# A graph-attention kernel on one core: a new written order for the steady slot, and 13 of 28 projection half passes back to 128 columns

## The chip, the cores and the metric

The kernel runs on 1 core of one Trainium2 chip. The metric is the time on the device in microseconds (us) of one execution. A core has five engines with queues of their own: TensorE (PE; its weight loads are listed as PEld), VectorE (DVE), ScalarE (ACT), GpSimd (POOL) and SyncE (SP, which only issues DMA transfers here). Each executes its own instructions in the order in which the program lists them, and waits on semaphores for the others.

## The reference

For each of 32 batches `b`, `x[b]` is 512 channels by 1024 nodes in float32. What is computed, cut to what matters:

```
q = wq . x          k = wk . x                    # per node
s[m, n] = leaky_relu(q[n] + k[m], 0.01)
att = softmax(s, over n)                          # 1024 x 1024 per batch
agg[c, m] = sum_n x[c, n] att[m, n]
y = layernorm(x + relu(adj @ agg + bm))           # layer 0; norm over the nodes
W = adj * adj
out = layernorm(y + W^T y + bias)                 # layer 1
```

## The kernel before, in words

**The attention without its matrix.** Because of leaky_relu, exp(s) is a product of a function of q and one of k on each side of a threshold. The kernel ranks the nodes by q, stores the projected rows z = (q, adj·x, k) in rank order in DRAM, makes prefix sums of exp(q)·z from both ends ("tables"), stores them too, and each node then fetches one row of three entries (prefix, own rank's row, suffix) and mixes them.

**The steps.** Everything that a batch needs is cut into named steps, and a text lists the steps of one "slot". In a slot several batches are at different stages: a step has a role (an offset to the slot's number), so slot s does the projection of batch s+2, the tables and fetches of batch s+1, the mixing and the layer-1 product of batch s, the last layernorm of batch s-1, and loads batch s+3. The list is the order in each engine's queue. One slot after the other makes the steady part. Names, in the order of one batch:

- `ld0..3` load x (SP). `x01..x04`, `x11..x14` (DVE, 128x512 subtractions and additions): operands of a Strassen-like product with seven products per half g; their place is in `y` for g = 0 and in rows 0 to 3 of the tile `rows` for g = 1.
- `p0..p27` (PE, L312, `project`): 28 half passes of 2 products with contraction 128, 257 columns moving. Results are collected in PSUM tiles of the tags A, B and C (each one buffer of two banks; T is the fourth tag). `k0p1 k0p5 k0u2 k021 k1...` (ACT, L333) and `k011 k012 k022 k111 k112 k122` (DVE, L331) bring them to `zrow`. `p12` can't write tag C before `k011` has read it, and `p15` can't write A before `k022`.
- `pk mx mr qb ql en`: maximum of q, q on all partitions (PE transposes). `r0..r7` (DVE, L377): ranks. `sd0..sd7` (POOL, L389): indirect DMA of `zrow` to DRAM in rank order. `fe` (SP, L435 and L440): the ranked rows back into `zs`, after all eight `sd`. `c0..c7` (ACT, L402): counts for each k.
- `wx0 wx1` (ACT, L450) and `wb0 wb1` (DVE, L462): weights of the tables, from the first column of `zs`. `t0..t8` (PE, L484, 64 columns): the tables, one after the other in tag T (`t8` in C); `e` (ACT, L496) reads each out, `ca` (ACT) and `cp` (POOL, L502) carry one row to the next, `ts` (SP, L510) stores it, by two DMAs.
- `pi0..pi7` (POOL, L517, indirect DMA into `rows`): each node's row, after the landing of all `ts`. `oa`, `no` (DVE, L532 on, L546 on), `ox`, `sh`, `sx`: the mixing factors; `oa0` needs `pi0` to `pi3`, `oa1` needs `pi4` to `pi7`. `sc` (ACT, L556) and `ga`, `gb` (DVE, L561): the mixing itself, for 8 groups of rows.
- `u0..u3` (PE, L568): 8 transposes each of all rows, so `u0` is behind the last `ga`/`gb`. They use tag C, so each waits for the `ad` of the one before. `ad` (DVE, L575), `sq` (ACT), `rt` (POOL), `y` (ACT, L600): layer 0's sum and layernorm.
- `T1..T4` (DVE, L624), `sA sB` (PE, L630, bias seeds), `m0..m13` (PE, L647, 128x128 weights, 512 columns moving), `rd...` (ACT L670, DVE L668): layer 1 by seven products.
- `st ro sf av so`: statistics (DVE), root (POOL), shift (DVE), application (ACT), store (SP).

**The half passes.** A product in `project` is made as two matmuls of 64 weight columns each, which go to the two halves of the output partitions:

```
        for c in range(2):
            for n in range(0, P, G):
                nc.tensor.matmul(
                    zp[n : n + G, m, 0:CE],
                    side(b, g, a)[:, c, m * P + n : m * P + n + G],
                    wb[:, w, c, :],
```

with P = 128, G = 64 and CE = 257. In the profile each float32 matmul shows as two records, so a half pass has 8 records.

**Order around it.** `begin()` and `opening()` make the first three batches' work by hand up to the first slot, `slot(s)` runs the list for s = 1 to 29 (the first copy of the list is run by `opening()`), and `end()` the last two batches by hand.

Of the kernel before, what the change touches and what calls it, by code (L numbers as in the profile page):

```python
# [23 lines left out]
def gat_gcn_resnorm_kernel(  # L24
# [141 lines left out]
    def turn_weights():  # L166
        pt = bank("T", [P, N], "pt_v")
        nc.tensor.transpose(pt[:, 0 : 3 * CT], vec, ident[0 : 3 * CT, 0 : 3 * CT])
        for i in range(2):
            nc.vector.tensor_copy(wb[:, 2 * i + 1, :, 0], pt[:, 2 * i : 2 * i + 2])  # L170
            nc.vector.tensor_copy(wb[:, 2 * i, :, CE - 1], pt[:, CT + 2 * i : CT + 2 * i + 2])
        nc.vector.tensor_scalar(nbm, pt[:, 2 * CT : 3 * CT], -1.0, None, ALU.mult)
        for ct in (2, 3, 0, 1):
            pt = bank("ABCT"[ct], [P, C], f"pt_{ct}")
            for ot in range(CT):
                nc.tensor.transpose(
                    pt[:, ot * P : (ot + 1) * P], adj_sb[:, ot, ct * P : (ct + 1) * P], ident
                )
            i = 2 * (ct // 2)
            nc.vector.tensor_copy(wb[:, i, ct % 2, 0 : CE - 1], pt[:, C // 2 : C])  # L180
            nc.scalar.copy(wb[:, i + 1, ct % 2, 1:CE], pt[:, 0 : C // 2])
        for to, of, less in ((4, 1, 0), (5, 3, 4), (6, 2, 5), (1, 3, 1)):
            nc.vector.tensor_tensor(wb[:, to], wb[:, of], wb[:, less], ALU.subtract)

    def seed_bias():
# [18 lines left out]
    def square_weights():  # L204


        nc.vector.scalar_tensor_tensor(w1, adj_sb, SC, adj_sb, ALU.mult, ALU.mult)
        for ct in range(CT):
            w = w1[:, ct, ct * P : (ct + 1) * P]
            nc.vector.scalar_tensor_tensor(w, ident, SC, w, ALU.mult, ALU.add)  # L210
        nc.vector.tensor_tensor(ws[:, 0], a21, a22, ALU.add)
        nc.vector.tensor_tensor(ws[:, 1], ws[:, 0], a11, ALU.subtract)
        nc.vector.tensor_tensor(ws[:, 2], a12, ws[:, 1], ALU.subtract)
        nc.vector.tensor_tensor(a21, a11, a21, ALU.subtract)
# [89 lines left out]
    def project(b, i):  # L304
# [4 lines left out]
        zp = held(zps, (b, g, at), lambda: bank(at, [P, 2, H], f"zp_{at}_{b}_{g}"))  # L309
        for c in range(2):  # L310
            for n in range(0, P, G):
                nc.tensor.matmul(  # L312
                    zp[n : n + G, m, 0:CE],
                    side(b, g, a)[:, c, m * P + n : m * P + n + G],
                    wb[:, w, c, :],
                    start=first and c == 0,
                    stop=c == 1,
                    skip_group_check=not first,
                )
# [26 lines left out]
    def spread(b, to="T"):  # L346

        qb = qbs[b] = bank(to, [P, N], f"qb_{b}")
# [216 lines left out]
    def turn(b, ot, at="C"):  # L565
        op = tops[b, ot] = bank(at, [P, N], f"op_{b}_{ot}")
# [139 lines left out]

    steps = {}
# [56 lines left out]
    for what in names:  # L764
        also(0, f"rd{what}", read, what)

# [10 lines left out]
    def run(s, plan, but=()):  # L777

        for name in plan.split():
            if name not in but:  # L780
                do(s + steps[name][0], name)

    def tables(b, *some):
        for k in some:
            do(b, f"t{k} e{k}")
            if k < NB - 1:
                do(b, f"cp{k} ca{k}")
            do(b, f"ts{k}")

    def gains(b, *some):  # L790
        do(b, " ".join(f"{g}{k}" for g in ("ga", "gb") for k in some))

    kept = {
        3: "k0p1 k011", 5: "k0p5", 7: "k0u2", 9: "k012", 11: "k022", 15: "k021",
        17: "k1p5", 19: "k1p1 k111", 23: "k1u2 k112", 25: "k122", 27: "k121",
    }

    def whole(b, before={}, after={}):

        do(b, "x01 x02 x04 x03 x11 x12 x14 x13")  # L800
        for i in range(NP):
            for f in before.get(i, ()):
                f()
            do(b, f"p{i} {kept.get(i, '')}")
            for f in after.get(i, ()):
                f()

    def begin():

        turn_weights()  # L810
        whole(0)
        square_weights()
        do(0, "pk")
        spread(0, "B")
        done.add(("qb", 0))
        do(0, "mx mr ql en")
        do(0, "r0 r1 sd0 sd1 r2 r3 sd2 sd3 r4 r5 sd4 sd5 r6 r7 sd6 sd7 fe")
        seed_bias()
        whole(
            1,  # L820
            before={
                21: (lambda: do(0, "wx0 wb0"),),
                24: (lambda: tables(0, 0),),
                26: (lambda: tables(0, 1), lambda: do(0, "wx1 wb1")),
            },
            after={
                i: (lambda z=z: do(0, f"c{z}"),) for z, i in enumerate((3, 7, 10, 14, 17, 21))
            },
        )
        do(1, "pk")  # L830
        spread(1, "B")
        done.add(("qb", 1))
        do(1, "mx mr ql en")

        def pair(nt):
            do(1, f"r{nt} r{nt + 1} sd{nt} sd{nt + 1}")

        def gather():
            do(0, "pi0 pi1 pi2 pi3")
            do(1, "fe")  # L840
            do(0, "pi4 pi5 pi6 pi7")

        whole(
            2,
            before={
                0: (lambda: pair(0), lambda: tables(0, 2), lambda: do(0, "c6")),
                2: (lambda: pair(4), lambda: tables(0, 3), lambda: do(0, "c7")),
                4: (lambda: pair(2), lambda: tables(0, 4), lambda: do(0, "sh sx")),
                5: (lambda: pair(6), lambda: tables(0, 5)),
                7: (lambda: tables(0, 6),),  # L850
                9: (lambda: tables(0, 7),),
                11: (lambda: tables(0, 8),),
                12: (gather,),
                13: (lambda: do(1, "c0 c1"),),
                16: (lambda: do(1, "c2 c3"),),
                19: (lambda: do(1, "c4 c5"),),
                23: (lambda: do(1, "c6 c7 wx0 wb0"),),
                25: (lambda: tables(1, 0),),
                27: (lambda: tables(1, 1),),
            },  # L860
        )

    def shares(b, h):
        do(b, f"oa{h} ox{h} no{h} " + " ".join(f"sc{k}" for k in range(4 * h, 4 * h + 4)))

    def opening():

        shares(0, 0)
        do(1, "wx1 wb1")
        gains(0, 0, 1)  # L870
        tables(1, 2)
        gains(0, 2, 3)
        tables(1, 3)
        shares(0, 1)
        gains(0, 4, 5, 6, 7)
        do(1, "sh sx")
        for ot in range(CT):
            turn(0, ot, "CA"[ot % 2])
            done.add((f"u{ot}", 0))
            tables(1, 4 + ot)  # L880
            do(0, f"ad{ot} sq{ot} rt{ot}")
            if ot > 0:
                do(0, f"y{ot - 1}")
# [185 lines left out]
```

## Time and profile before

| | us |
|---|---|
| median of 3 runs | 2316.03 (2310.62 to 2318.45) |
| the profiled execution | 2319.07 |
| its span, from first to last instruction | 2317.4 |
| PE busy | 2141.9 (92%) |
| DVE busy | 1806.8 (78%) |
| ACT busy | 1648.0 (71%) |
| POOL busy | 1020.2 (44%) |
| mean granted TensorE clock | 0.973 of full speed; 1.00 in the ten windows of the steady part that were looked at |

Some groups of instructions, by line and shape (mean ns of one):

| step | shape | count | mean ns |
|---|---|---|---|
| p, zp_A from x, L312 matmul | 128 rows, 64 columns, 257 moving | 2048 | 387 |
| p, its weight load | 128x64 | 2048 | 138 |
| t, L484 matmul | 128 rows, 64 columns, 257 moving | 2304 | 402 |
| m, oA from y, L647 matmul | 128x128, 512 moving | 768 | 601 |
| m, its weight load | 128x128 | 768 | 192 |
| u, L568 transpose | 128x128, 128 moving | 1024 | 283 |
| u, its weight load | 128x128 | 1024 | 143 |
| ga, gb, L561 | 128x512 | 512 | 778 |
| st, L676 (two per step) | 128x512 | 240 | 676 |
| r, L377 | 128x1024 | 240 | 1281 |
| sd, L389 | indirect DMA | 256 | 1252 |
| pi, L517 | indirect DMA | 256 | 1079 |

Matmul records overlap, and their ends are modelled: what a step costs on PE is read from the distance of starts, not from the mean duration. "Busy" for PE is therefore no measure of how close it is to its limit. A slot can be marked by the first transposes of L568, which occur once in a slot behind all mixing; in the time from 255 us to 2155 us the single transpose of L357 (step `mx`) returns every 66 to 71 us.

### The profile page before, as it was taken

The numbers are of one execution on the slowest core, as the hardware profiler recorded it, in microseconds if no ns is written. First come the engines' busy times: TensorE is split into PE (matmuls) and PEld (weight loads), VectorE is DVE, ScalarE is ACT, GpSimd is POOL, SyncE is SP. The second block draws the span as 40 slices with busy tenths as digits, with TensorE's granted clock in tenths as the row PEclk, the third lists the DMA queues.
The fourth block names the chain that finished last, engine by engine and source line by source line (L and its number), as shares of the span: only waits on it lengthen the run. The fifth ranks groups of instructions, "written<-read, shape, count | busy, mean of one in ns | idle before, by whom it ended". The sixth has DMA issues, their size and how long they took to land.

```text
span 2317.4 us, 37553 instructions
## 1 busy us (share of the span) xinstructions
PE 2141.9 (92%) x12689; PEld 1204.2 (52%) x12721; DVE 1806.8 (78%) x3574; ACT 1648.0 (71%) x2758; POOL 1020.2 (44%) x1293
## 2 busy tenths in 40 slices
PE   6669999999999999999999999999999999999776
PEld 4334555555555555555555555555555555555332
DVE  6537888788888888878788878888888888888555
ACT  1357778777777877677787777877777777777654
POOL 1225444444544444455444455444445544444431
PEclk9879999999999999999999999999999999999878
DMA  6357777777877777887777787777778777778641
GB/s 237 95 192 238 259 243 246 239 249 253 270 259 243 247 236 254 248 269 247 236 233 252 239 274 261 240 234 244 244 249 283 258 231 238 249 248 269 223 175 72
DMA packets 178774, 548.96 MB, mean 237 GB/s; under 512 B 27020, under 2 KB 27032, under 8 KB 178584
## 3 DMA queue, kind: packets, MB, share of 16 engines
q1 hardware_dynamic: 121216, 277.05, 40.8%
q0 software_dynamic: 57344, 269.52, 33.2%
q8 instruction: 101, 1.65, 0.3%
q14 instruction: 89, 0.73, 0.1%
q10 hardware_dynamic: 24, 0.01, 0.0%
HBM read 338.17 MB, written 208.30 MB: 236 GB/s over the span
## 4 chain that ended last, share of the span: by engine, by line
PE 39%; DMA 23%; DVE 8%; ACT 7%; issue 7%; POOL 5%; SPq 2%; POOLq 0%; DVEq 0%; ACTq 0%
PE tp L484 11%; DMA rows<-td,idx 11%; PE zp_A L312 10%; PE op L568 6%; DMA zs<-td 5%; PE zp_B L312 4%; PE oA L647 4%; DMA td<-zrow,ranki 3%; POOL rows L517 3%; DMA td<-zs 2%; POOL td L389 2%; DVE st L676 2%; DMA x<-in_x_dram 2%; ACT x L584 2%; DVE rows L561 2%
## 5 line engine op out<-in xcount | busy, mean ns | idle before, releaser
L484 PE MATMUL tp<-zs,lq 128*64 128x257 f32 x2304 | 364.6, 402 | 60.9 <-POOL zs L502 37.4
L389 POOL DMA_INDIRECT td<-zrow,ranki x256 | 320.4, 1252 | 198.2 <-DVE ranki L382 97.1
L561 DVE SCALAR_TENSOR_TENSOR rows<-rows,ra 128x512 f32<-128x512 f32 x512 | 380.4, 778 | 19.1 <-ACT rows L556 15.8
L647 PE MATMUL oA<-y,adj_sb 128*128 128x512 f32 x768 | 352.4, 601 | 6.9 <-DVE v L668 2.4
L377 DVE SCALAR_TENSOR_TENSOR junk<-qb,zrow,first 128x1024 int8<-128x1024 f32 x240 | 307.5, 1281 | 18.1 <-DMA out_dram<-v 7.5
L517 POOL DMA_INDIRECT rows<-td,idx x256 | 276.2, 1079 | 92.7 <-issue 68.0
L312 PE MATMUL zp_A<-wb,x 128*64 128x257 f32 x2048 | 280.9, 387 | 27.5 <-DVE zrow L331 26.0
L502 POOL COPY zs<-ts 1x513 f32<-1x513 f32 x128 | 81.8, 639 | 457.6 <-ACT ts L496 457.6
L484 PEld LDWEIGHTS tp<-zs,lq 128*64 128x64 f32 x2304 | 184.0, 140 | 187.1 <-POOL zs L502 63.6
L575 DVE SCALAR_TENSOR_TENSOR y<-op,nbm,x 128x1024 f32<-128x1024 f32 x128 | 164.0, 1284 | 149.9 <-PE op L568 148.1
L402 ACT ACTIVATE junk<-lq,kc 128x1024 int8<-128x1024 f32 x240 | 274.3, 1143 | 1.9
L647 PEld LDWEIGHTS oA<-y,adj_sb 128*128 128x128 f32 x768 | 145.1, 192 | 190.0 <-issue 149.0
L312 PEld LDWEIGHTS zp_A<-wb,x 128*64 128x64 f32 x2048 | 165.2, 138 | 106.0 <-DVE zrow L331 42.0
L502 POOL COPY zs<-zs 1x513 f32<-1x513 f32 x128 | 78.8, 615 | 268.6 <-ACT zs L496 268.6
L333 ACT COPY zrow<-zp_A 128x514 f32<-128x514 f32 x192 | 112.6, 586 | 112.4 <-PE zp_A L312 94.5
L556 ACT ACTIVATE rows<-rows,ra 128x512 f32<-128x512 f32 x256 | 175.6, 713 | 4.3 <-DVE ra L549 4.3
L670 ACT COPY v<-oA 128x1024 f32<-128x1024 f32 x90 | 89.8, 998 | 107.9 <-PE oA L647 97.2
L600 ACT ACTIVATE y<-y,nb,r 128x1024 f32<-128x1024 f32 x128 | 158.9, 1242 | 4.3
L312 PE MATMUL zp_C<-wb,x 128*64 128x257 f32 x1024 | 147.0, 388 | 15.9 <-DVE zrow L331 15.4
L700 ACT ACTIVATE v<-v,nb,rs 128x1024 f32<-128x1024 f32 x120 | 148.6, 1238 | 13.7 <-DVE nb L692 11.7
L568 PE MATMUL op<-ident,rows 128*128 128x128 f32 x1024 | 148.3, 283 | 9.6 <-DVE rows L561 7.2
L676 DVE BATCH_NORM_STATS2 st<-v 128x6 f32<-128x512 f32 x240 | 152.1, 676 | 0.0
(163 smaller groups left out, 3858.0 us busy)
## 6 DMA issues: line engine op xcount, KB each, us to landing
x<-in_x_dram SPq DMA_DIRECT2D x128, 512.0 KB
out_dram<-v SPq DMA_DIRECT2D x120, 512.0 KB
zs<-td SPq DMA_DIRECT2D x64, 602.3 KB
td<-zs SPq DMA_DIRECT2D x288, 120.2 KB
td<-ts SPq DMA_DIRECT2D x224, 120.2 KB
zs<-td SPq DMA_DIRECT2D x64, 240.9 KB
zs<-td SPq DMA_DIRECT2D x96, 120.5 KB
td<-zs SPq DMA_DIRECT2D x8, 514.0 KB
```

What stands on the lines that cost most here:

```text
L312: nc.tensor.matmul(zp[n : n + G, m, 0:CE], side(b, g, a)[:, c, m * P + n : m * P + n + G], wb[:, w, c, :], start=first and c == 0, stop=c ...
L377: nc.vector.scalar_tensor_tensor(junk(b)[:, 0:N], qbs[b], zrow[:, nt, 0:1], first[:, o : o + N], ALU.subtract, ALU.is_lt, accum_out=rank[: ...
L389: sc = nc.gpsimd.indirect_dma_start(out=td[:, :], out_offset=bass.IndirectOffsetOnAxis(ap=ranki[:, nt : nt + 1], axis=0), in_=zrow[:, nt, ...
L402: nc.scalar.activation(junk(b)[:, N : 2 * N], qs[b], AF.Sign, bias=kcs[b][:, nt : nt + 1], accum_out=signs(b)[:, nt : nt + 1],)
L484: nc.tensor.matmul(tp[i * G : (i + 1) * G, h, 0:CE], lw[:, ks[i], :], zs[:, j, 1 + h * CE : 1 + (h + 1) * CE], start=True, stop=True,)
L517: nc.gpsimd.indirect_dma_start(out=rows[:, mt, :], out_offset=None, in_=tdb[b % 2].rearrange("(s u) c -> s (u c)", u=3), in_offset=bass.In ...
L556: nc.scalar.activation(u, u, AF.Copy, scale=ratios(b)[:, k, 1:2])
L561: nc.vector.scalar_tensor_tensor(u, rg[:, k, i, 1 : C + 1], ratios(b)[:, k, i : i + 1], u, ALU.mult, ALU.add)
L568: nc.tensor.transpose(op[:, mt * P : (mt + 1) * P], rg[:, mt, 1, 1 + ot * P : 1 + (ot + 1) * P], ident)
L575: nc.vector.scalar_tensor_tensor(yall[:, ot], tops.pop((b, ot)), nbm[:, ot : ot + 1], xs[b][:, ot], ALU.max, ALU.add, accum_out=sm,)
L647: nc.tensor.matmul(o[:, m, :], quarters[w][:, a, m * P : (m + 1) * P], part(b, y)[:, a, :], start=fresh and a == 0, stop=a == CT // 2 - 1, ...
L676: nc.vector.bn_stats(st[:, h, :], vs[b][:, mt, h * H : (h + 1) * H])
```

## The change

It replaces the list of the steady slot by another one with the same steps (none is added or left out), and it makes `project` choose its form by a second list: the half passes in `NARROW` keep two 64-column matmuls per product, the other 13 (p1 to p4 and p19 to p27) make one matmul of 128 columns. The hand-written `begin()`, `opening()` and `end()` become lists as well (`BEGIN`, `END`), and helper functions are cut into steps for this; the order of their steps stays, apart from the one copy of the slot's list that each holds, which follows the new list, and `wb0` of the last batch, which goes from POOL to DVE.

```diff
         zp = held(zps, (b, g, at), lambda: bank(at, [P, 2, H], f"zp_{at}_{b}_{g}"))
+        wide = G if f"p{i}" in NARROW.split() else P
         for c in range(2):
-            for n in range(0, P, G):
+            for n in range(0, P, wide):
                 nc.tensor.matmul(
-                    zp[n : n + G, m, 0:CE],
-                    side(b, g, a)[:, c, m * P + n : m * P + n + G],
+                    zp[n : n + wide, m, 0:CE],
+                    side(b, g, a)[:, c, m * P + n : m * P + n + wide],
                     wb[:, w, c, :],
...
     SLOT = """
-    ga3 st1 p4 p1 st0 p3 p2 ga2 ro0 ga0 p0 k0p1 st2 p5 p7 k0p5 gb0 ro2 p6 k011 ro1 sf2 ga1 p12 k0u2
-    st3 av2 p8 p11 oa1 ro3 sf1 p10 ox1 av1 no1 p9 sf0 k022 sc6 sc5 p15 k012 ga5 p14 wx0 wb0 sc4 x11
-    t0 k021 gb1 p19 sf3 e0 gb5 sc7 cp0 ts0 ga6 p17 ca0 ga4 so1 av3 t1 gb2 gb6 p16 e1 wx1 p18 cp1 ts1
-    wb1 ca1 k1p1 t2 x12 gb3 p13 e2 ga7 p23 ca2 cp2 ts2 gb7 av0 k111 t3 k1p5 gb4 u0 e3 p22 ca3 cp3
-    ad0 k1u2 t4 x13 sq0 u1 p24 e4 ld0 ad1 so0 ca4 cp4 p25 so2 rt0 x14 sq1 t5 k122 sh u2 e5 ld1 rt1
-    ts3 y0 p20 ad2 cp5 p21 ca5 sq2 t6 k112 p27 e6 sB ca6 cp6 ts6 u3 y1 rt2 ts5 t7 ad3 so3 ts4 p26 e7
-    pk ld2 mx ca7 cp7 qb ts7 mr k121 sq3 t8 r0 sA r1 e8 m1 rt3 y2 ts8 en ld3 T1 sd0 ql m0 y3 r2 sd1
-    m3 c0 T2 pi2 sx m2 r3 rdp1 pi0 c1 r4 pi3 m5 rdp5 r5 pi1 m7 T3 sd3 m4 r6 r7 m6 rdu2 c2 sd6 m9
-    rd11 c3 sd5 T4 m8 pi7 x01 oa0 m11 pi5 rd22 ox0 c4 no0 sd4 c5 m10 x02 sd7 sc0 m12 c6 x03 sd2 rd12
-    sc3 m13 sc2 pi4 x04 pi6 rd21 sc1 c7 fe
+    ga2 st1 p4 p1 ga3 p2 ga0 st3 p3 p5 k0p1 gb3 ro3 p6 k0p5 st0 p7 st2 p0 ro0 k0u2 p9 gb0 ro2 p10
+    sf3 gb2 ro1 p11 sf0 oa1 av0 k011 p8 k022 ox1 av3 so0 p12 no1 p15 x11 sc5 p14 wx0 wb0 sc4 t0 k012
+    k021 ga1 p17 e0 gb1 ca0 p19 cp0 ts0 ga4 sc6 sf2 x12 t1 sc7 ga5 p16 ga7 e1 p18 wx1 sf1 cp1 ts1
+    wb1 ca1 k1p1 t2 gb7 av2 gb4 p13 e2 ga6 ca2 p23 cp2 k111 av1 gb5 t3 gb6 k1p5 so1 u0 x14 so3 e3
+    so2 ca3 p22 cp3 ad0 t4 k1u2 x13 sq0 u1 p25 e4 ad1 ca4 cp4 ts4 p24 rt0 sq1 t5 u2 e5 rt1 y0 p21
+    ts5 ad2 cp5 p20 ld0 ca5 ts2 k122 sq2 t6 k112 ld1 pk u3 sh e6 ld2 ca6 p27 cp6 ad3 y1 t7 mx p26 e7
+    mr T1 ca7 cp7 ts7 qb sq3 ts6 t8 r0 ts3 sB rt3 e8 r1 m3 k121 ts8 rt2 ld3 en y2 sd0 m2 y3 pi1 sA
+    m1 ql T2 pi2 T3 pi0 m0 r2 pi3 m7 rdp1 r3 rdp5 m5 T4 sd2 c0 r4 pi5 c1 m4 r5 sd1 m6 rdu2 r6 sd3 c2
+    m8 r7 sd4 c3 x01 pi7 m11 c4 oa0 rd11 sd5 ox0 c5 m9 x02 sd7 sx c6 no0 m10 sd6 rd22 sc0 sc2 m12
+    pi6 x03 sc3 x04 pi4 rd12 m13 rd21 c7 sc1 fe
     """
 
+    NARROW = "p0 p5 p6 p7 p8 p9 p10 p11 p12 p13 p14 p15 p16 p17 p18"
```

## The prediction

> **What bounds the kernel now.** First the page, for the span and the slices:
>
> ```profile
> span 2317.4 us, 37553 instructions
> PE 2141.9 (92%) x12689; PEld 1204.2 (52%) x12721; DVE 1806.8 (78%) x3574; ACT 1648.0 (71%) x2758; POOL 1020.2 (44%) x1293
> PE   6669999999999999999999999999999999999776
> ```
>
> PE looks like the bound, and 33 of 40 slices are steady. The timeline of one slot shows where it isn't (PE, then the waits of the other engines):
>
> ```profile
> 1067.66 1.04 PE L350 MATMUL qb<-ident,zrow 128*128 128x128 f32 x8
> 1068.63 1.09 PE L484 MATMUL tp<-zs,lq 128*64 128x257 f32 x8
> 1069.65 0.60 PE L630 MATMUL oA<-seeds,ones 128*128 128x512 bf16 x2
> 1070.09 3.60 PE L647 MATMUL oA<-y,adj_sb 128*128 128x512 f32 x8
> ...
> 1075.83 1.05 POOL L517 DMA_INDIRECT rows<-td,idx  x1 [0.58 <-issue]
> 1079.80 2.05 POOL L517 DMA_INDIRECT rows<-td,idx  x1 [0.30 <-issue]
> 1088.60 0.16 DVE L532 TENSOR_TENSOR s<-rows,kc 128x4 f32<-128x4 f32 x1 [1.44 <-DMA rows<-td,idx]
> 1096.44 1.01 POOL L517 DMA_INDIRECT rows<-td,idx  x1 [0.30 <-issue]
> 1106.57 0.16 DVE L532 TENSOR_TENSOR s<-rows,kc 128x4 f32<-128x4 f32 x1 [2.43 <-DMA rows<-td,idx]
> 1108.93 1.96 PE L312 MATMUL zp_A<-wb,x 128*64 128x257 f32 x16 [2.58 <-DVE zrow L331]
> 1110.09 0.67 ACT L450 ACTIVATE w<-zs,bw,el 128x2 f32<-128x2 f32 x2 [0.36 <-DMA zs<-td]
> 1110.86 1.36 PE L484 MATMUL tp<-zs,lq 128*64 128x257 f32 x8
> ```
>
> And the same slot by stages, from its `u0` (1052.49) on:
>
> ```profile
> 1052.49:1058.49 6.00, 6.00 (x51) 3.99 (x52) 4.23 (x7) 5.03 (x11) 1.59 (x3) 1.00 0.11 10
> 1058.49:1074.49 16.00, 15.95 (x105) 9.81 (x103) 10.76 (x25) 15.32 (x26) 7.03 (x13) 1.00 0.91 309
> 1074.49:1102.49 28.00, 27.61 (x119) 13.42 (x119) 25.28 (x46) 17.95 (x31) 21.17 (x21) 1.00 0.89 308
> 1102.49:1110.49 8.00, 5.42 (x50) 3.36 (x48) 4.87 (x16) 3.86 (x7) 1.44 (x3) 1.00 1.01 214
> 1110.49:1120.20 9.71, 9.64 (x77) 6.28 (x75) 9.53 (x18) 8.09 (x15) 1.88 (x3) 1.00 0.49 144
> ```
>
> (Columns: length, busy PE, PEld, DVE, ACT, POOL, clock, DMA share, GB/s.) PE loses 2.6 us in the fourth stage, where the DMA engines are full (1.01); in the first and last they are nearly free (0.11, 0.49). The slot is a loop through all engines, and I count it from `u0`, averaged over 23 slots, 67.95 us: `u0` to `t8` 16.1 (PE); `e8`, `ts8` and its landing; four fetches on POOL; they land, and `oa0` starts at 36.6. From there DVE has no slack until the last `gb`, and the next `u0` waits for that. Start distances price DVE: `ga`/`gb` 0.70, `st` 1.44, `x` and `k` 0.60, wide adds (`rd`, `T`) 1.15, `oa` 0.56, `no` 0.71, `wb0` 0.50, `wb1` 1.34, `sf` 0.10. In the old order what follows `oa0` sums to 29.5; 36.6 + 29.5 leaves 1.85 of DVE idle in 67.95, which are waits such as the 2.43 above for the last four fetches.
>
> **The change, part by part.**
>
> *The form.* Narrow half passes start 0.87 apart; 8 records in pairs, 0.214 a pair. No 128-column float32 matmul with 257 moving columns is in the trace. By the nearest row, `m` (0.4285 from start to start for 512 columns), a wide record takes 0.215, four of them 0.86: equal. The far end is that the 128-column load (0.192 in `m`) isn't hidden: 4 x (0.214 + 0.192) = 1.62, or 13 x 0.76 = 9.9 us in a slot; below nothing, only the few records less, which PE doesn't wait for. I take 0.86: in `m` each load begins with the matmul before it and has 0.215 to hide in, and `u` has 128x128 loads and matmuls every 0.109.
>
> *The switches.* `qb`, whose neighbour before is wide, lasts 0.97, and `t8` behind it 1.02, where alone they need 0.87 each. Over many pairs a change of form costs about 0.10 before and 0.05 behind: 0.15. The old slot has 12 changes on PE; I count 16 in the new one (`p3`|`p5`, around `p19`, around `p23` are new; `u0`-`p22`, `u1`-`p25` and their like only move them). That is 4 x 0.15 = 0.6 us a slot on PE. The Trainium skill (TensorEngine Tiling, Key Properties) says that changing the tiling mode drains the TensorE. The trace agrees (0.15 a change), and the rule alone speaks against this change; its result is a rival below. I cost the switches at nothing: `p3`|`p5` lies in a stage where PE waits for DVE, and `p19` and `p23` lie between tables `t0` to `t3`, where `t2` waits for `wb1`. Without that cover they cost the 0.6.
>
> *`sB` goes behind `t8`.* The seeds of tag B (0.44) stood in the stretch from `u0` to `t8`, which is PE's alone. `t8`, `e8`, `ts8` are 0.44 earlier. `ts8` is now behind `ts6` and `ts3` on SP; a `ts` holds SP 0.85 (two issues, four took 1.70). `ts7` can go at 14.5 after `u0`, the two are through at 17.1, and `e8` ends at 17.7 (18.14 before): not late.
>
> *Fetches.* POOL's order was `sd0 sd1 pi2 pi0 pi3 pi1`, and is `sd0 pi1 pi2 pi0 pi3`. They are issued 1.31 apart, so the four end 1.31 earlier, with 0.44 from above: `oa0` at 36.6 - 1.75 = 34.85. Bounds: 36.6 if full DMA engines (0.89) eat it all, 34.1 if the stores moved away (below) shorten `ts8`'s landing too (4.0 now). I take 34.85, since a queue that starts earlier with the same bytes ends earlier. The last scatter, fourteenth of sixteen as before, goes at 37.2 after `u0` instead of 40.7: no more POOL gaps waiting for `r`, whose list loses `T1` and `rd11`. Behind it `pi6` and `pi4` go at 38.5 and 39.8, before at 42.1 and 43.5. `fe` waits for the landing of all scatters (46.7 now), so the fetch of `zs` starts about 2.5 earlier, and `wx0` could start near 54 instead of 56.5.
>
> *DVE.* `T1` goes into the `u` stage (idle DVE there, 4.85 us a slot waiting for transposes), `x04` ahead of `m13`'s end, `rd11` behind `oa0`: after `oa0` DVE has 30.65, which is 1.15 more than before (`rd11`). Idle in it: the last four fetches took some 10.1 from `pi6` (1096.44) to `oa1` (1106.57); 39.8 + 10.1 = 49.9, and DVE gets to `oa1` at 34.85 + 16.5 = 51.3: no wait left. `k011` and `k022` stand behind `oa1` now, at 52.4 and 53.0; PE, with `p4` at 42.4, is at `p12` at 53.0: no stall. On ACT `wx0` now queues behind `av0`, `ox1`, `av3` and `sc5`; by their rows (1.2, 0.2, 1.2, 0.67) it ends at 55.4, where DVE has come to `wb0` at 54.4: 1.0 idle. Sum for DVE: 34.85 + 30.65 + 1.1 = 66.6.
>
> *PE in the last stage.* `t0` at 55.9 (57.5 before). `t2` is behind `wb1`, at 62.75; `t3` 2.9 later (`p13`, `p23`, two changes); `u0` 1.05 behind it: 66.7. The two ways agree, and the later sets the slot: 66.7, that is 1.25 less than 67.95.
>
> *Stores.* `so2` and `so3` were issued in the full stage after `u0`; now three `so` (512 KB each) go around `u0`, where DMA has 0.11 to 0.49. The loads `ld0` and `ld1` go some 3 us later, and are needed only by `x01`, at 33. I count nothing for it.
>
> *Begin and end.* Written out as lists with the same order; the wide form there adds some dozen changes (2 us), where PE is 60 to 70% busy. Nothing, give or take 5.
>
> **Sum:** 29 spacings of slots x 1.25 = 36 us. The profiled execution has 2319.07 (2317.4 and 1.7 around it): 2283. The median of the runs is 3.0 below it, so 2280.
>
> **The rivals.**
>
> *More than that.* If the four fetches land 0.75 earlier still and DVE never idles, a slot is 34.1 + 30.65 = 64.75: 3.2 x 29 = 93 us, about 2223; three quarters of it is 2246, the low end of the range. Against it: 1.85 of idle now, in an order that has as many handovers to ACT.
>
> *Nothing.* DMA moves the same bytes, and from 6 to 58 us of the slot it is 0.9 to 1.0 busy. If the landings stay where they are, `oa0` is at 36.6 and `oa1` at 53; DVE has 13.9 behind `oa1`, `u0` at about 68: 2316. For it: a wait of 2.43 on DMA. Against: the full stretch begins with what POOL and SP are given, and that is earlier.
>
> *Slower: the switches are paid.* Here PE's path sets the slot: `t0` doesn't come earlier, and `p19` and `p23`, alone among 64-column work, lengthen the links `t0`-`t1` and `t2`-`t3` by 0.3 each. Place: the ten us before `u0`. It decides as soon as the landings give less than 0.6 to `t0`. Price 0.6 x 29 = 17 us: 2333. This is the result that the rule of the Trainium skill would give by itself. For it: `t0` to `u0` is 10.4 in the old slot, all table chain. Against: `t2` waits for weights anyway.
>
> *Slower: loads that show.* A wide half pass above 0.86 counts in the `u` stage, which holds seven of the 13 and is PE's alone. At 0.95 it is 0.6 a slot, at the far end 5.3: from 2300 to 2430.
>
> **How the numbers follow.** Forecast 0.56 (own range 2262 to 2302), more 0.10, nothing 0.09, switches paid 0.16, loads that show 0.09. A measurement of this kernel tells about 0.3% (7 us) from no change. Faster: 0.55 of the forecast's share, 0.10, and 0.02 of the loads, 0.67; within 0.3%: 0.09; slower: 0.24. The range 2245 to 2336 leaves out half of "more", most of "loads" and tails.
>
> **What would show it.** Right: `mx` returns every 66 to 67 us; `oa0` is near 35 us behind `u0`, `oa1` no longer waits for DMA; wide half passes start 0.86 apart; PE's waits for `zrow` L331 shrink. Wrong: wide half passes well over 0.87; `p12` waiting for `k011`; DVE idle before `T2` growing into `sd` issues that end later than 38; `t0` later than 56 behind `u0`.

## The result, and the profile after

The changed kernel takes 2295.39 us (median of 4 runs, 2290.95 to 2295.52), the kernel before, run beside it, 2315.4: a ratio of 0.9911, 95% interval 0.989 to 0.9932. The change makes the kernel faster by some 20 us; 2280 was forecast, so the sign held and the size was 15 us too large. The profiled executions, which the rest goes by, have 2319.07 and 2295.47. (Of the run with all half passes narrow, below, one execution took 2323.83 us, over 1% longer than its five others; it is left out of the ratio there, and its trace is not read.) Cut at `u0` of every slot, the two traces give:

| stretch | before, us | after, us | difference |
|---|---|---|---|
| start to the first `u0` | 163.0 | 163.4 | +0.4 |
| first slot | 77.5 | 76.3 | -1.2 |
| 28 steady slots, mean of one | 67.82 | 66.80 | 28 x -1.02 = -28.5 |
| `u0` of batch 29 to that of batch 30 | 82.6 | 88.0 | **+5.4** |
| the next | 40.3 | 39.3 | -1.0 |
| last `u0` to the end | 55.0 | 56.4 | +1.4 |
| span | 2317.4 | 2293.8 | -23.6 |

So two things are to be explained: where the 1.02 us of each slot come from, and what costs 5.4 us at the end. The page of the changed kernel, span, busy times and PE's slices:

```profile
span 2293.8 us, 34082 instructions
...
PE 2118.9 (92%) x11025; PEld 1234.7 (54%) x11057; DVE 1796.0 (78%) x3576; ACT 1663.7 (73%) x2758; POOL 994.0 (43%) x1291
...
PE   6669999999999999999999999999999999999676
```

The shares say nothing of it: 92% and 78% as before. The slices show one thing: near the end, in the third from the right, PE has 6 tenths instead of 7. One slot by stages, from its `u0` (841.14) on (length, busy PE, PEld, DVE, ACT, POOL, clock, DMA share, GB/s):

```profile
841.14:847.14 6.00, 6.00 (x42) 4.51 (x42) 3.88 (x7) 5.08 (x11) 1.90 (x4) 1.00 0.73 283
847.14:863.14 16.00, 15.34 (x86) 9.75 (x84) 9.84 (x23) 14.84 (x25) 6.90 (x12) 1.00 0.77 234
863.14:891.14 28.00, 27.07 (x94) 13.72 (x94) 25.81 (x47) 17.93 (x31) 17.51 (x19) 1.00 0.92 324
891.14:899.14 8.00, 8.00 (x78) 5.25 (x74) 6.87 (x20) 5.66 (x10) 2.37 (x4) 1.00 0.98 226
899.14:908.01 8.87, 8.58 (x61) 4.87 (x57) 8.87 (x16) 8.38 (x14) 2.08 (x3) 1.00 0.23 74
```

In the fourth stage PE was busy 5.42 of 8.00 us and is busy 8.00 of 8.00 now. The first stage, where the DMA engines were nearly free (0.11), is at 0.73: three stores have moved there; the second has come down from 0.91 to 0.77. The same slot on the timeline (start, duration, engine, line, and in brackets the idle time before and what ended it):

```profile
855.49 1.22 DVE L642 TENSOR_TENSOR rows<-y 128x1024 f32<-128x1024 f32 x1
855.49 1.69 POOL L518 COPY zs<-zs 1x513 f32<-1x513 f32 x1 [2.15 <-ACT zs L512]
857.23 1.09 PE L500 MATMUL tp<-zs,lq 128*64 128x257 f32 x8 [0.50 <-POOL zs L518]
862.64 1.97 POOL L533 DMA_INDIRECT rows<-td,idx  x1 [1.35 <-PE oB L665]
876.64 0.16 DVE L548 TENSOR_TENSOR s<-rows,kc 128x4 f32<-128x4 f32 x1 [1.68 <-DMA rows<-td,idx]
880.82 3.70 PE L665 MATMUL oA<-y,adj_sb 128*128 128x512 f32 x8 [0.93 <-DVE v L686]
892.70 0.16 DVE L548 TENSOR_TENSOR s<-rows,kc 128x4 f32<-128x4 f32 x1
896.39 0.65 ACT L466 ACTIVATE w<-zs,bw,el 128x2 f32<-128x2 f32 x2
897.53 1.04 PE L500 MATMUL tp<-zs,lq 128*64 128x257 f32 x8
```

The first fetch starts 21.5 after `u0` (862.64) instead of 23.4, `oa0` (876.64) still waits for the fetched rows, `oa1` (892.70) no longer waits for anything, and `t0` (897.53) follows without a gap. What `oa0` and `oa1` wait for over the whole run, before and after (us in all, number of waits):

```profile
L532 DVE TENSOR_TENSOR s<-rows,kc x64: 149/164/206, 151.5 to 2257.2; 128x4 f32<-128x4 f32 x64
...
DMA rows<-td,idx: 81.0, 44
```

```profile
L548 DVE TENSOR_TENSOR s<-rows,kc x64: 147/161/168, 151.9 to 2232.0; 128x4 f32<-128x4 f32 x64
...
DMA rows<-td,idx: 50.2, 32
```

These two steps lost 30.8 us less of DVE's time on fetched rows; the 28 slots are 28.5 us shorter. The gain of a slot goes with a shorter wait for fetched rows. That the two sums are nearly equal does not show that one is the other: DVE has a new wait, for ACT ahead of `T2` (79.8 us in the run), and `rd11` early, below, takes another 29.4 us off the wait for rows (20.8) without a shorter slot that could be seen. Why the rows come earlier, and which of the many moves did it, the trace alone can't say. The steps, counted from `u0`, means over 23 slots:

| step | before | foretold | after |
|---|---|---|---|
| `t8` on PE | 16.13 | 15.7 | 16.09 |
| first fetch on POOL | 23.39 | - | 21.59 |
| `oa0` | 36.61 | 34.85 | 35.16 |
| last scatter | 40.73 | 37.2 | 38.32 |
| the last two fetches | 42.08, 43.48 | 38.5, 39.8 | 39.60, 41.06 |
| `oa1` | 52.99 | 51.3 | 51.46 |
| `k022` | 54.60 | 53.0 | 52.95 |
| `t0` | 57.46 | 55.9 | 56.19 |
| slot, the same 23 | 67.97 | 66.7 | 66.72 |
| slot, all 28 | 67.82 | - | 66.80 |

### The profile page after: what moved, and what is told of

It is laid out like the page before. It is cut to its first block, busy times and chain, and to the rows that moved or that the text cites. A ratio compares the mean times of both kernels' runs of the same rounds, so it can differ in the third digit from the quotient of the medians.

```text
span 2293.8 us, 34082 instructions
## 1 busy us (share of the span) xinstructions
PE 2118.9 (92%) x11025; PEld 1234.7 (54%) x11057; DVE 1796.0 (78%) x3576; ACT 1663.7 (73%) x2758; POOL 994.0 (43%) x1291
## 4 chain that ended last, share of the span: by engine, by line
PE 43%; DMA 16%; ACT 13%; DVE 7%; issue 7%; POOL 5%; SPq 1%; POOLq 0%; DVEq 0%; ACTq 0%
PE zp_A L328 12%; DMA rows<-td,idx 10%; PE tp L500 9%; PE oA L665 6%; PE zp_B L328 6%; PE zp_C L328 4%; ACT x L602 3%; ACT y L618 3%; PE op L586 3%; ACT zs L512 3%; POOL rows L533 3%; DMA zs<-td 2%; POOL zs L518 2%; DMA td<-zs 2%; DVE v L686 2%
## 5 line engine op out<-in xcount | busy, mean ns | idle before, releaser
L500 PE MATMUL tp<-zs,lq 128*64 128x257 f32 x2304 | 345.5, 404 | 80.8 <-POOL zs L518 47.9
L665 PE MATMUL oA<-y,adj_sb 128*128 128x512 f32 x768 | 359.2, 604 | 24.4 <-DVE v L686 20.6
L577 DVE SCALAR_TENSOR_TENSOR rows<-rows,ra 128x512 f32<-128x512 f32 x512 | 371.9, 761 | 4.1 <-ACT rows L572 3.1
L533 POOL DMA_INDIRECT rows<-td,idx x256 | 294.3, 1149 | 116.1 <-issue 71.0
L405 POOL DMA_INDIRECT td<-zrow,ranki x256 | 265.0, 1035 | 156.8 <-DVE ranki L398 56.5
L500 PEld LDWEIGHTS tp<-zs,lq 128*64 128x64 f32 x2304 | 164.6, 140 | 224.4 <-POOL zs L518 102.4
L518 POOL COPY zs<-ts 1x513 f32<-1x513 f32 x128 | 86.5, 676 | 446.8 <-ACT ts L512 446.8
L328 PE MATMUL zp_A<-wb,x 128*64 128x257 f32 (+1 forms) x1408 | 258.6, 383 | 1.6 <-DVE zrow L347 1.6
L518 POOL COPY zs<-zs 1x513 f32<-1x513 f32 x128 | 110.1, 860 | 278.2 <-ACT zs L512 278.1
L328 PEld LDWEIGHTS zp_A<-wb,x 128*64 128x64 f32 (+1 forms) x1408 | 171.3, 162 | 57.3 <-ACT ts L512 11.2
L328 PE MATMUL zp_B<-wb,y 128*64 128x257 f32 (+1 forms) x896 | 136.5, 389 | 15.5 <-DVE y L317 15.5
```

What stands on the lines that cost most here:

```text
L328: nc.tensor.matmul(zp[n : n + wide, m, 0:CE], side(b, g, a)[:, c, m * P + n : m * P + n + wide], wb[:, w, c, :], start=first and c == 0, s ...
L405: sc = nc.gpsimd.indirect_dma_start(out=td[:, :], out_offset=bass.IndirectOffsetOnAxis(ap=ranki[:, nt : nt + 1], axis=0), in_=zrow[:, nt, ...
L500: nc.tensor.matmul(tp[i * G : (i + 1) * G, h, 0:CE], lw[:, ks[i], :], zs[:, j, 1 + h * CE : 1 + (h + 1) * CE], start=True, stop=True,)
L518: copy(zs[row : row + 1, to, 1:ZW], ts[row : row + 1, 0 : ZW - 1])
L533: nc.gpsimd.indirect_dma_start(out=rows[:, mt, :], out_offset=None, in_=tdb[b % 2].rearrange("(s u) c -> s (u c)", u=3), in_offset=bass.In ...
L577: nc.vector.scalar_tensor_tensor(u, rg[:, k, i, 1 : C + 1], ratios(b)[:, k, i : i + 1], u, ALU.mult, ALU.add)
```

## The experiments

The kernel before had medians of 2315.7 to 2318.1 beside these runs. The table collects what the traces of the experiments show of a slot; the length of a slot is the mean of 28, the steps are means of 23, idle is DVE's wait for fetched rows ahead of `oa1`, landing that of the last fetch (not in every trace).

| kernel | time, us | ratio (95%) | slot | first fetch | `oa0` | `oa1` (idle) | last fetch, landing |
|---|---|---|---|---|---|---|---|
| before | 2315.4 | 1 | 67.82 | 23.39 | 36.61 | 52.99 (0.82) | 43.48, - |
| changed | 2295.4 | 0.9911 (0.989 to 0.9932) | 66.80 | 21.59 | 35.16 | 51.46 (0.06) | 41.06, 50.12 |
| changed, again | 2302.1 | 0.993 (0.9908 to 0.9953) | 66.85 | 21.65 | 35.34 | 51.59 (0.08) | 41.26, 50.16 |
| old list, 13 wide | 2321.3 | 1.002 (1.0005 to 1.0035) | 67.85 | 23.23 | 36.14 | 52.55 (0.86) | 43.10, - |
| `wb0` of batch 31 on POOL | 2304.4 | 0.9947 (0.9933 to 0.9961) | 67.27 | 21.60 | 35.24 | 51.94 (0.20) | 41.68, - |
| T1 later | 2304.7 | 0.9946 (0.9927 to 0.9965) | 66.95 | 21.43 | 34.69 | 51.86 (1.00) | 42.28, - |
| sd1 first | 2297.1 | 0.9907 (0.9877 to 0.9938) | 66.88 | 21.85 | 35.46 | 51.58 (0) | 40.71, 49.45 |
| rd11 early | 2302.7 | 0.9938 (0.991 to 0.9965) | 66.68 | 21.54 | 35.27 | 51.34 (0.01) | 41.44, 50.39 |
| stores late | 2339.5 | 1.0096 (1.0062 to 1.013) | 68.22 | 22.85 | 36.17 | 52.64 (0.19) | 42.39, 51.60 |
| old list, stores early | 2312.8 | 0.9987 (0.9971 to 1.0004) | 67.71 | 23.05 | 36.08 | 52.61 (0.97) | 43.60, 52.30 |
| cp7 on ACT | 2288.4 | 0.9888 (0.9866 to 0.9911) | 66.44 | 21.40 | 34.56 | 50.97 (0.23) | 41.48, 50.36 |
| pi5 late | 2304.3 | 0.9938 (0.9917 to 0.9959) | 67.04 | 21.56 | 35.22 | 51.57 (0.23) | 41.86, 50.94 |
| three mends | 2294.5 | 0.9913 (0.9893 to 0.9932) | 66.87 | 21.48 | 35.33 | 51.49 (0.09) | 41.73, 50.62 |

### The form alone: all half passes narrow, and the old list with 13 wide

The new list with no wide half pass:

```diff
-    NARROW = "p0 p5 p6 p7 p8 p9 p10 p11 p12 p13 p14 p15 p16 p17 p18"
+    NARROW = "p0 p1 p2 p3 ... p27"
```

> The new list with all 28 half passes in the 64-column form: the form alone is undone. PE then has 14 changes of form in a slot instead of 16. Theory (the new order makes the gain, and a change of form of 0.15 us is hidden): the same time as the changed kernel within 5 us, 2290 to 2300, with 1 us or more less in a slot than before. Rival (the changes around p19 and p23 are paid): 0.6 us less in each of 30 slots, 2277. Rival (the wide form itself makes the gain): the gain is gone, 2310 or more.

Measured: 2296.64 us, ratio 0.9906 (0.9889 to 0.9923), the changed kernel's time.

The old list with the form of the new kernel:

```diff
+        wide = G if 0 == i or 4 < i < 19 else P
...
-            for n in range(0, P, G):
+            for n in range(0, P, wide):
```

> The kernel before with its old list and only the form changed: p1 to p4 and p19 to p27 wide. 16 changes of form in a slot instead of 12. Theory (the form is no gain and its changes are mostly hidden): 2312 to 2322. Rival (they are paid): 0.6 us in each of 30 slots, 2333. Rival (the form makes the gain): 2300 or less.

Measured: 2321.29 us, 1.002 (1.0005 to 1.0035); the mean slot is 67.85, as before. The form makes no gain in either list, and costs little: the old list loses 0.2%, 5.6 us, where four more changes of form at 0.15 in 29 slots would be 17. Where the 5.6 are lost, one trace of each can't tell. So the gain of the changed kernel is that of the new list. In the changed kernel's trace a wide half pass stands beside a narrow one at the same price. PE on the timeline, two stretches of the slot of above:

```profile
853.65 1.09 PE L500 MATMUL tp<-zs,lq 128*64 128x257 f32 x8
854.67 0.32 PE L373 MATMUL mx<-ident,q 128*128 128x128 f32 x1
...
884.36 1.03 PE L328 MATMUL zp_B<-wb,y 128*128 128x257 f32 x4
885.23 1.03 PE L328 MATMUL zp_C<-wb,x 128*128 128x257 f32 x4
886.09 1.90 PE L328 MATMUL zp_A<-wb,x 128*128 128x257 f32 x8
```

From start to start a wide half pass takes 0.87 and 0.86 (the mean is 0.87), four records instead of eight; the 64-column table between two 128-column neighbours takes 1.02. A change of form costs 0.10 before and 0.05 behind, in both kernels (0.10 behind where a wide half pass follows a narrow one: `p19` and `p23`, alone between narrow work, take 1.07). The slot has 12 changes before and 16 after, as counted in the forecast.

### batch 31's block products on POOL again

```diff
-    def weigh_by(b, part, by=nc.vector):
+    def weigh_by(b, part):
+        by = nc.gpsimd if b == B - 1 and part == 0 else nc.vector
```

> The changed kernel with one step put back: wb0 of the last batch on POOL, as before, so that the last four fetches of batch 30 wait behind it. Theory (the copy of the list in the end is longer since the four fetches now fill the DMA engines while the last zs is read back): the stretch from the u0 of slot 29 to that of slot 30 falls from 88.0 to about 82, the read-back of zs from 15 us to 6, and the time by 5 us, to 2290. Rival (the end is longer for another reason, such as DVE held by wb0): the stretch stays within 1 us of 88, and so does the time.

Measured: 2304.41 us, 0.9947 (0.9933 to 0.9961): not the time that was expected, so the times don't show this gain. But the stretch in question went from 87.97 to 82.56 us, as before the change. The rest of this execution is longer (start 166.8, first slot 79.3, slots 67.27), and of that the edit touches nothing. What it does at the end is seen on POOL and ACT. The changed kernel, timeline, then its waits in that stretch (us, times, longest):

```profile
2146.69 1.04 POOL L533 DMA_INDIRECT rows<-td,idx  x1 [0.30 <-issue]
...
2149.81 0.66 SPq L451 DMA_DIRECT2D zs<-td  x2
...
2150.64 0.99 POOL L533 DMA_INDIRECT rows<-td,idx  x1 [0.30 <-issue]
...
2165.22 0.67 ACT L466 ACTIVATE w<-zs,bw,el 128x2 f32<-128x2 f32 x2 [9.50 <-DMA zs<-td]
```

```profile
PE tp L500 <- DVE lq L478: 13.1, 1, 13.1
ACT w L466 <- DMA zs<-td: 9.5, 1, 9.5
```

And this experiment, timeline of ACT and POOL:

```profile
2176.61 0.67 ACT L466 ACTIVATE w<-zs,bw,el 128x2 f32<-128x2 f32 x2 [1.25 <-DMA zs<-td]
2178.15 1.07 POOL L534 DMA_INDIRECT rows<-td,idx  x1 [0.30 <-issue]
```

With `wb0` on DVE, POOL has nothing to wait for, and the four last fetches of batch 30 go out (2146.7 to 2150.6) just as SP begins to read batch 31's rows back (2149.8). The read-back then takes until 2165.2, 15.4 us; with `wb0` on POOL the fetches queue behind it, go out after the read-back (2178.2), and the read-back takes 7.1 (from 2169.5), in the kernel before 6.1 (2179.9 to 2186.1). PE has nothing else to do there, so it waits 13.1 for the weights. POOL's wait for `wb0` was what kept the two transfers apart. Every kernel here with `wb0` on DVE has 85.9 to 88.0 in this stretch, every one with it on POOL 81.8 to 82.8.

### T1 later

`T1` goes back to where the old list had it (behind `en`), with the seeds and products exchanged so that the order stays valid; `k121` moves up.

```diff
-    mr T1 ca7 cp7 ts7 qb sq3 ts6 t8 r0 ts3 sB rt3 e8 r1 m3 k121 ts8 rt2 ld3 en y2 sd0 m2 y3 pi1 sA
-    m1 ql T2 pi2 T3 pi0 m0 r2 pi3 ...
+    mr ca7 cp7 ts7 qb k121 sq3 ts6 t8 r0 ts3 sA rt3 e8 r1 m1 ts8 rt2 ld3 en T1 y2 sd0 m0 y3 pi1 sB
+    m3 ql T2 pi2 T3 pi0 m2 r2 pi3 ...
```

> The changed kernel with T1 moved behind t8 (after en), so that m1 and m0 with sA come ahead of sB, m3 and m2, and k121 ahead of sq3. Theory (POOL's copy cp7 takes 1.7 us instead of 0.6 since it waits for T1 on DVE, and t8 waits for cp7): cp7 is back at 0.6, t8 starts 15.5 us behind u0 instead of 16.1, its wait for the row is gone, and a slot is 0.3 to 0.6 shorter: 2278 to 2287. Rival (DVE's work behind the fetched rows sets the slot whatever t8 does, and T1 is back where DVE is full): t8 is earlier but the slot is the same, 2292 to 2300.

Measured: 2304.74 us, 0.9946 (0.9927 to 0.9965), the slot 66.95. Two effects that cancel. First, `cp7`, by groups of line L502 (before) and L518 (changed, then this kernel; busy, mean ns | idle):

```profile
L502 POOL COPY zs<-zs 1x513 f32<-1x513 f32 x128 | 78.8, 615 | 268.6 <-ACT zs L496 268.6
```

```profile
L518 POOL COPY zs<-zs 1x513 f32<-1x513 f32 x128 | 110.1, 860 | 278.2 <-ACT zs L512 278.1
```

```profile
L518 POOL COPY zs<-zs 1x513 f32<-1x513 f32 x128 | 80.0, 625 | 277.9 <-ACT zs L512 277.9
```

The change lengthened this group by 31 us: one copy in four, `cp7`, takes 1.69 instead of 0.61, because `T1` now runs beside it (855.49, above). With `T1` elsewhere it is 0.61 again, `t8` starts at 15.53 instead of 16.09, and `oa0` is 0.47 earlier. Second, `T1` stands in front of the ranks again: `r7` is 0.6 later, the last scatter behind it 0.7, the last fetch 1.2 (42.28), and `oa1` waits 1.00 for its rows, as much as in the kernel before (0.82). What came in at `oa0` went out at `oa1`.

### The changed kernel again, sd1 first, rd11 early, stores late

> The changed kernel unaltered, beside the next ones on the same chip. The kernels with batch 31's block products on POOL and with T1 later came out at 2304 us, 9 above the changed kernel's 2295, and their records are longer already in the first slots, which no edit of theirs touches (first transposed row at 166.8 and 167.1 us after the start, against 163.4). If that is the chip or the moment, this run gives some 2300 to 2305 too; if it is their edits, it gives 2295 again.

Measured: 2302.12 us (2297.49 to 2307.51), ratio 0.993 (0.9908 to 0.9953), slots of 66.85. So the two 2304 above are within what the unaltered kernel shows on another occasion, and times taken on different occasions are not compared below some 7 us. The slots of the traces are no finer a measure: the steady list of the changed kernel was traced three times, and a slot had 66.80, 66.85 and, in the run with `wb0` of batch 31 on POOL, 67.27. So a difference of less than 0.5 between two traces shows nothing. Single steps are steadier in the three: `t8` 16.09 to 16.10, the first fetch 21.59 to 21.65, `oa0` 35.16 to 35.34.

```diff
-    ... y2 sd0 m2 y3 pi1 sA m1 ... r5 sd1 m6 ...
+    ... y2 sd0 m2 y3 sd1 pi1 sA m1 ... r5 m6 ...
```

> One step moved back: sd1 ahead of pi1 again, in the 28 steady slots, everything else as changed. If the slot's gain comes from the scatter that no longer stands ahead of four picks, their landings and oa0 fall back by some 1.3 us and the slot by up to 1.0: 28 x (0.7 to 1.0), 20 to 28 us more than the changed kernel. If the DVE's chain of work ahead of oa0 (T1, then T2 behind y3) makes the gain instead, oa0 moves by less than the 1.35 us of idle time that stands ahead of it and the time changes by less than 6 us.

Measured: 2297.14 us, no loss; the first fetch is 0.26 later, `oa0` 0.30, the slot 0.08 at most, which is within the spread. The scatter that the prediction paid 1.31 for is worth next to nothing in the new list.

```diff
-    m8 r7 sd4 c3 x01 pi7 m11 c4 oa0 rd11 sd5 ...
+    m8 r7 sd4 c3 rd11 x01 pi7 m11 c4 oa0 sd5 ...
```

> rd11 goes from behind oa0 to right behind r7, everything else as changed. DVE is idle for 1.35 us a slot ahead of oa0, and rd22, which m12 waits for (0.95 us a slot on PE), stands behind rd11. If DVE's chain from oa0 to oa1 carries the slot, 0.4 to 0.6 us a slot go, 11 to 17 us less than the changed kernel. If the landings of pi6 and pi4 (50.1 us into the slot, against oa1 at 51.5) or the residual fetch carry it, less than 4 us go. If x01 and oa0, now one operation later on POOL or DVE, are late for it, up to 10 us more.

Measured: 2302.65 us; the slot 66.68, 0.12 to 0.17 less than the changed kernel's two traces, which neither the times nor the traces can tell from nothing. `oa0` is where it was (35.27), since it waits for fetched rows. What DVE waits for ahead of the first instruction of `no` (L562), in the changed kernel and then here (us, times):

```profile
ACT ac L442: 1.2, 3
```

```profile
ACT ac L442: 28.4, 29
```

Behind `oa0`, `rd11` had covered the time until ACT has made the mixing factors of `sx`; without it DVE waits 1.00 there in every slot. So its 1.2 us were not on the path.

```diff
-    ... av3 so0 p12 ... k1p5 so1 u0 x14 so3 e3 so2 ca3 ... e4 ad1 ca4 cp4 ts4 p24 ... cp6 ad3 y1 ...
+    ... av3 p12 ... k1p5 u0 x14 e3 ca3 ... e4 ad1 so0 ca4 cp4 ts4 so1 p24 so2 ... cp6 ad3 so3 y1 ...
```

> The four stores of a batch's output go out later (so0 from between p8 and p12 to behind ad1, so1 to behind ts4, so2 behind p24, so3 behind ad3), everything else as changed. The prediction costed the stores' place at nothing. By that, less than 4 us either way. The rival is that loads and stores share the DMA engines with the spread of the scores (ts8) and the picks: then ts8's rows or the first picks land later and oa0 goes from 35.2 us into the slot to as much as 36, and the time up by 5 to 20 us.

Measured: 2339.52 us, 1.0096 (1.0062 to 1.013), 37 us more than the changed kernel beside it, nearly twice what even the rival had allowed. The slot is 1.4 us longer. On SP's queue the four stores of a slot now go out at -4.9, 5.5, 5.9 and 11.5 us from `u0`, in the changed kernel at -14.0, -0.3, 0.1 and 0.6, in the kernel before at -7.4, 4.9, 5.5 and 13.7: so three of them stand among the table stores again, as they did before. Why: what POOL waited for ahead of the fetches, in the changed kernel and then here (us, times):

```profile
PE oB L665: 33.6, 24
DMA zs<-td: 5.1, 1
DMA td<-zs: 2.6, 3
DMA x<-in_x_dram: 1.7, 1
```

```profile
DMA td<-zs: 31.7, 13
DMA x<-in_x_dram: 27.8, 9
DMA zs<-td: 5.2, 1
PE oB L665: 1.3, 2
```

In the changed kernel a batch's first fetch waits for PE's last reading of `rows` (a product ends 21.15 into the slot, the fetch starts at 21.6); the last table rows had landed at 20.6. With the stores late it waits for transfers of SP's queue: the last rows are issued at 18.85 instead of 18.22, land at 21.8, and the fetch starts at 22.85 (what takes the last 1.0 is not shown). From issue to landing, the median of a table store is 3.6 and 4.2 us (its two kinds) instead of 2.1 and 2.8. One us at the first fetch is one us at `oa0` (36.17), and at least as much at the slot's end.

### The old list with early stores

```diff
-    ... av3 t1 gb2 ... wb1 ca1 ... gb7 av0 k111 ... ad1 so0 ca4 cp4 p25 so2 rt0 ... ad3 so3 ts4 ...
+    ... av3 t1 so3 gb2 ... wb1 so2 ca1 ... gb7 av0 so0 k111 ... ad1 ca4 cp4 p25 rt0 ... ad3 ts4 ...
```

> The kernel before, with three of its four stores a slot moved forward (so3 from behind ad3 to behind t1, so2 from behind p25 to behind wb1, so0 from behind ad1 to behind av0), and nothing else of the change. Putting the stores late in the new list cost 1.4 us a slot, with the first pick 1.26 us later. If that is where the gain of the new list comes from, the old list gets most of it from this alone: the first pick goes from 23.4 us into the slot to 22.2 or less, the slot from 67.8 us to some 66.8 to 67.2, the time down by 17 to 28 us. If in the old list sd1 ahead of the picks (POOL is taken by it until 23.1) holds them anyway, the first pick moves by 0.3 us at most and the time by less than 8 us.

Measured: 2312.81 us, 0.9987 (0.9971 to 1.0004). The second case, to the number: the first fetch is 0.34 earlier, at 23.05 in every slot, since POOL is taken until 22.75. The table rows do come earlier: their last packets end at 20.5 instead of 21.8, and they have landed at 21.1. And of what is gained at `oa0` (0.53) 0.38 are left at `oa1`, which waits 0.97 for a last fetch that is issued no earlier (43.60), and 0.1 to 0.2 at the end of the slot. Why POOL is taken so long in the old list, the kernel before shows (timeline of POOL and DVE, the slot that begins at 1531.01):

```profile
1550.25 1.22 DVE L624 TENSOR_TENSOR rows<-y 128x1024 f32<-128x1024 f32 x1
1550.63 1.84 POOL L389 DMA_INDIRECT td<-zrow,ranki  x1 [1.00 <-DVE zrow L344]
1552.78 0.99 POOL L389 DMA_INDIRECT td<-zrow,ranki  x1 [0.31 <-issue]
1554.59 1.05 POOL L517 DMA_INDIRECT rows<-td,idx  x1 [0.82 <-DMA x<-in_x_dram]
```

`sd0` starts 0.6 later than in the new list and, beside `T1`, takes 1.84 instead of 1.13; so `sd1` ends at 22.75 into the slot, in the new list with `sd1` first at 21.44. The first fetch here waits a little longer still (0.82) for a transfer. Two conditions, POOL free and table rows landed, ended within some half a microsecond of each other: POOL at 22.8, the rows at about 22.4 (an estimate: their last packets end at 21.8, and from there to the landing it is 0.5 to 0.6 in the traces that show both). Moving the stores alone is worth some 4 us in the old list (2316.57 beside it; the interval leaves room for none and for 7); freeing POOL alone was not run there. The new list has moved both.

### cp7 on ACT

```diff
-            also(1, f"cp{k}", carry, k, 0, nc.gpsimd)
+            also(1, f"cp{k}", carry, k, 0, nc.scalar if k == 7 else nc.gpsimd)
```

> The changed kernel with one copy a slot, cp7, on ACT instead of POOL. On POOL it takes 1.69 us instead of 0.60, while T1 runs on DVE, and t8 waits for it; on ACT it runs behind ca7, 0.62 us each. t8 should start at about 15.6 us into the slot instead of 16.1, ts8 and the first pick 0.4 earlier, and if the picks' start carries on to the slot's end as with the stores, the slot is 0.2 to 0.45 us shorter: 6 to 13 us. If the picks are held by the DMA engines behind that, t8 moves and the time stays within 4 us.

Measured: 2288.44 us, ratio 0.9888 (0.9866 to 0.9911) to the kernel before, the fastest here; by the traces the slot has 66.44, 0.36 to 0.83 less than the changed list's three, and the span is 11 and 13 us less than in the changed kernel's two. `t8` starts at 15.62, the first four fetches are on average 0.4 earlier, `oa0` 0.60. So the copy beside `T1` is what held `t8`. The ranks are not as early as in the changed kernel: `T2` waits 3.1 instead of 2.6 a slot for ACT, which now has the copy, and `r7` is at 32.04 instead of 31.58; but the last fetches are hardly later, and `oa1` waits 0.23 where `T1` later had 1.00. That this kernel is faster than the changed one is likely and not shown: the interval touches that of the changed kernel, and 0.36 is within the spread of its slots.

### pi5 late

```diff
-    ... T4 sd2 c0 r4 pi5 c1 ... c4 oa0 rd11 ...
+    ... T4 sd2 c0 r4 c1 ... c4 oa0 pi5 rd11 ...
```

> The changed kernel with one fetch later: pi5 from behind r4 (issued 29.0 us into the slot) to behind oa0, where the old list has it; the scatters behind it on POOL come 1.3 us earlier for it, and the first four fetches stay as they are. If the gain needs the last fetches to land early too, so that oa1 doesn't wait (the last lands at 50.1, oa1 is at 51.5; in the old order 52.3 and 52.6), the last landing goes to 52 or later, oa1 waits again and the slot is 0.6 to 1.2 us longer: 17 to 34 us. If only the first four fetches and oa0 make the gain, the time stays within 6 us.

Measured: 2304.31 us, slots of 67.04. Neither case: the last fetch is issued and lands 0.8 later, not 2, and `oa1` waits 0.23; the slot is 0.2 longer, which neither the times nor the traces can tell. The landing has 1.3 us of room before `oa1`, and this used 0.8 of it.

### Three mends at once

`cp7` on ACT, `rd11` behind `r7`, and `wb0` of batch 31 on POOL, as in the diffs above.

> The changed kernel with three edits at once: cp7 on ACT, rd11 right behind r7, and the last batch's first block products on POOL as before the change. Each alone as far as run: POOL took 5.4 us from the end stretch in its trace, rd11 0.1 us a slot. With cp7's 6 to 13 us, 2282 to 2290 if they add up; within 5 us of the changed kernel if what they make room for goes into transfers.

Measured: 2294.47 us, 0.9913 (0.9893 to 0.9932). They don't add up. The end stretch has 81.75 us, 5.0 less than with `cp7` on ACT alone, but the slot has 66.87, 0.43 more, just less than three traces of one list differ by. The steps show a reason all the same. `oa0` is at 35.33 with DVE idle for only 0.08 ahead of it, where `cp7` alone gives 34.56: once the rows land early enough, `rd11` in front of `oa0` is on the path. And behind `oa0` DVE waits 1.0 for `sx`, as with `rd11` early alone. So `rd11` behind `oa0`, as the change has it, is the better place by these steps. `cp7` on ACT with `wb0` on POOL and without the `rd11` move was not run.

## Why the prediction was right, and where it wasn't

**The form and the changes of form**: right. A wide half pass costs 0.87 (0.86 foretold), a change 0.15, and in the new list nothing of it can be seen at the end: all-narrow takes the same time. The rivals "switches paid" and "loads that show" are out. The Trainium skill (TensorEngine Tiling (Array Packing), Key Properties) says that a change of tiling mode drains the TensorE; the 0.15 a change agrees with that, and the slower kernel that the rule alone would give did not come.

**`sB` behind `t8`, 0.44 earlier**: it failed. The reasoning about PE was right, since `t8` starts at 15.53 or 15.62 when `cp7` is out of `T1`'s way. But the change puts `T1` beside `cp7`, which the step did not look at: another 1.08 us on POOL, and `t8` stays at 16.09. A new wait took the place of the work removed.

**Fetches, "one scatter less, 1.31 earlier"**: the result was about right (`oa0` 35.16 against 34.85), the working not, and that the two agree is luck: 1.75 was forecast from two items, of which `sB` gave nothing and `sd1` in its old place costs 0.3 at `oa0` in the new list and no measurable time, and the rest of the 1.45 that came is from what was counted at nothing. What moves the first fetch by 1.8 is that several conditions for it come earlier together: the table rows (behind the stores) and POOL (`sd0` sooner, and without `T1` beside it). The step took the queue's length for the bound, and in the new list queue (20.2), landing (20.6) and PE's reading of `rows` (21.15) end within 1 us of each other. How the 1.8 divides between rows and POOL was not taken apart.

**Stores, "I count nothing for it"**: wrong, and the largest error of working. In the new list their place is worth 1.0 us at `oa0` and 1.4 us a slot (in the old one, with POOL taken, 0.1). The step also missed `so0`, which left the stage of the table stores as well: three stores left it, not two. The gain had been named as the far bound of `oa0` (34.1); the step then looked at the DMA share of the stage that the stores go to, and not at the table rows that stand behind them on SP's queue in the stage that they leave.

**Last scatters and fetches, no wait at `oa1`**: right, with two thirds of the size. The last scatter is 2.4 earlier (3.5 foretold), the last fetches 2.4 (3.6 foretold), `oa1` stands at 51.46 (51.3 foretold) with a wait of 0.06, and the reason given, `T1` out of the ranks' way, is shown by putting it back: the last fetch is 1.2 us later, and a wait of 1.00 is there again. The other 1.2 was not taken apart. Two of the forecast's own signs of being wrong came up narrowly: DVE waits 2.6 a slot ahead of `T2` and the last scatter goes at 38.3 (the limit was 38), and `t0` is at 56.19 (the limit was 56).

**From `oa1` to `u0`**: right. `k022` at 52.95 (53.0), `t0` at 56.19 (55.9), `u0` at 66.72 (66.7); this stretch is 15.3 us over the 23 slots, 0.3 longer than before, where the forecast had 0.4. PE's wait for `zrow` ahead of tag A fell from 26.0 us to 1.6, as foretold.

**The sum**: over the 23 slots that the forecast was worked out on it is met, 67.97 before and 66.72 after, 1.25 less. To the hundredth that is luck, with single slots between 66.2 and 70.8 before. The other five steady slots have 67.1 and 67.2 and gave nothing, so the mean of all 28 fell by 1.02. The 28 steady slots give 28.5 and the first one, the 29th spacing of the forecast, 1.2: 29.7 of the 36.

**Begin and end, "nothing, give or take 5"**: the size failed, just outside its bound. `wb0` on DVE frees POOL, the four fetches meet the read-back, +5.4; with the other pieces outside the slots (+0.4, -1.0, +1.4) the sum is +6.1. The step counted changes of form there and did not look at `wb0`, whose wait on POOL was what kept two transfers apart. So of the forecast's 36 us, 6.3 were not there in the slots, and 6.1 were given back outside them: 23.6 are left, in the profiled executions.

## What to carry to other kernels

Where a step has several conditions, list all with their end times before one is moved: here POOL's queue, the landing of rows and a reader on PE ended within 1 us, and moving one alone showed nothing (stores early in the old list: 0.1 us a slot less; `sd1` first in the new one: 0.1 more) while spoiling one cost 1.4. A large transfer has no price where it stands in the engine's share of busy time, but it has one for the small transfer behind it that something waits for. And when an engine is freed from a wait, look what it will issue sooner, and into which transfer that runs.

## What the hardware showed that was not expected

A DVE addition with both operands in SBUF holds up POOL. `cp7` (one row, 0.61 us) takes 1.69 when `T1` (1.22) starts at the same time, in 28 slots. The Trainium skill (SBUF — State Buffer, Who interferes with whom) says that a DVE instruction with two SBUF inputs contends with a GpSimd instruction that reads SBUF, and that the second of the two blocks; the trace agrees, 1.08 us late beside an addition of 1.22. POOL's indirect DMA instructions show the same: in the kernel before, the 74 scatters that start while an addition of L624 (1024 columns, both operands in SBUF) runs take 1.71 on average, the 48 that start during one of L668 (as many columns, one operand in PSUM) and meet none of L624 take 1.01.

Four indirect fetches sent out over 4 us ahead of and into a read-back on another queue made this 15.4 us instead of 6 to 7.
